# Both ends of a graph-attention kernel: a tile-wise start with three weight sums on GpSimd, row statistics on ScalarE, and a rearranged last block

## The chip, the cores and the metric

The kernel runs on one core of a Trainium2 chip, all in float32. The metric is the device time of one execution in microseconds (us). Lower is better. Before the change it was 2791.11 us, the median of 3 runs (2790.47 to 2792.8). Faster or slower needs a difference of 2%, which is 56 us here. The change aims at far less, so most of this study is about single microseconds, and about which of them are the kernel's and which are chance.

The engines are called as in the profile: PE (matmuls), DVE (vector), ACT (scalar), POOL (GpSimd), SP (issues transfers). Ratios are the mean time of one kernel's fast runs over the mean of the other's fast runs of the same rounds, so they are not quite the ratio of the medians quoted beside them.

## The reference, cut to what matters

```python
h = jnp.maximum(_layernorm(x, axis=-1), 0.0)          # x: 128 x 64 x 768, cut into 16 blocks of 512 rows
for l in range(2):
    m_left  = einsum('bsh,oh->bso', h, W_left[l])     # 768 x 768 weights
    m_right = einsum('bsh,oh->bso', h, W_right[l])
    u = ...                                           # h @ m_left^T, h @ m_right^T / sqrt(768), masked by adj
    attention = exp(u) * adj / (row sum + 1e-10)
    h_lin = einsum('bsh,oh->bso', h, W_lin[l]) + b_lin[l]
    h = relu(_layer_norm(attention @ h_lin, ln_a[l], ln_b[l]))
return x + h
```

## The kernel before: the parts that matter

Each 768x768 weight is cut into 3x3 blocks of 256, and a fast matrix-product scheme forms 15 block products from sums of weight blocks (`w_l`, `w_r`) and sums of token blocks (`ts`). I call the 15 products of block 0's left weight P0 to P14; the 15 of its right weight follow, then block 1. A product is added into bank X, Y, Z or V of PSUM, and "reads" by ACT and DVE gather the banks into `m`. The work beside the matmuls is hung on numbered slots of the product loop (`put(slot, ...)`, two slots a product).

The start (cut):

```python
# block 0: for each of four 128-row tiles q: statistics (DVE), root (ACT), inverse and shift (DVE), norm (ACT)
for q in range(Q):
    todo.extend(stats[q + 1:q + 2] + [scales[q], norms[q]])
...
def turn(c0):                     # two 128-column chunks of ALL four tiles: needs the last norm
    for c in range(2):
        for q in range(Q):
            nc.tensor.transpose(p[:, c, q * P:(q + 1) * P], xr[q][...], ident)
    ... nc.scalar.copy(ht[...], p[...])
...
t, w = deque(sums_t((1, 0, 0), nc.vector)), deque(sums_w(0, "l", nc.vector))     # all sums on DVE
needs = ("twww", "t", "wt", "ttwww", "wwww", "w", "tw", "t", ...)                # which sums before which product
# GpSimd: the 17 w_r sums for the right half, held back to slot 16
put(16, hold)
for n in range(0, len(rs), 3):
    put(17 + n // 3, *rs[n:n + 3])
```

Block 1's rows get their statistics on DVE during P8 to P13, are normalised on ACT, transposed on DVE, stored to DRAM as `h` and read back as `ht` (I call this the reload). GpSimd then makes the first token sums of block 1.

The end: the last block is computed in two halves of its rows. After each half its attention context is formed on PE, then squares and root on ACT, scaling on DVE, the addition of `ln_b` on GpSimd, relu and residual on DVE, and four stores on one queue.

## Time and profile before

| what | before |
|---|---|
| time, median of 3 | 2791.11 us |
| span of the profiled execution | 2791.6 us |
| PE busy | 99% of the span |
| first product P0 | 20.57 us |
| block 1's first product | 81.17 us |
| from the last half's first product to the end | 2791.6 - 2756.80 = 34.8 us |

Two views: the table of PE's waits, which tells for whom PE stood idle and how long, and the timeline, in which each row is a run of like instructions, with the start, the time from the first's start to the last's end, the count, and in brackets the idle time before it with what ended it.

### The profile page before, as it was taken

To read this page: it belongs to the slowest core of one execution; us is meant where nothing else is said; L and a number is where in the kernel's file an instruction comes from. 1 tells how busy PE (TensorE), PEld (TensorE's weight loads), DVE (VectorE), ACT (ScalarE), POOL (GpSimd) and SP (SyncE) were. 2 spreads that over 40 slices of the span, in tenths; PEclk is the share of its full clock that TensorE was granted. 3 is DMA by queue.
4 is the path that set the end of the run, shared out by engine and by line. 5 is a ranking of instruction groups with operands and counts; after the bars stand their busy time and mean duration, and the time that the engine had idled before them with its cause. 6 is when DMAs were issued, how large, how long until landed. Compare 5 with 4: busy or idle time off the path is not lost.

```text
span 2791.6 us, 46094 instructions
## 1 busy us (share of the span) xinstructions
PE 2751.3 (99%) x18712; PEld 2340.8 (84%) x18712; DVE 1340.8 (48%) x2215; ACT 837.8 (30%) x1453; POOL 1191.5 (43%) x935
## 2 busy tenths in 40 slices
PE   7999999999999999999999999999999999999997
PEld 6888888888888888888788888888888888888885
DVE  6455545454444332332345444544444335666666
ACT  2122222222231244444521211222121214445443
POOL 3332343223322456556432344223222325887875
PEclk9999999999999999999999999999999999999999
DMA  5533443344332243343555433443344204555654
GB/s 165 152 83 74 108 111 77 74 97 121 79 74 76 84 140 110 113 149 106 149 134 128 116 78 74 97 120 79 74 92 120 62 25 146 167 167 159 184 162 125
DMA packets 234068, 310.80 MB, mean 111 GB/s; under 512 B 54144, under 2 KB 184448, under 8 KB 225664
## 3 DMA queue, kind: packets, MB, share of 16 engines
q1 hardware_dynamic: 233568, 307.06, 41.5%
q8 instruction: 149, 2.44, 0.4%
q10 hardware_dynamic: 288, 0.79, 0.1%
q14 instruction: 63, 0.52, 0.1%
HBM read 202.91 MB, written 104.86 MB: 110 GB/s over the span
## 4 chain that ended last, share of the span: by engine, by line
PE 95%; issue 1%; DVE 1%; POOL 1%; DMA 1%; ACT 1%; SPq 0%; DVEq 0%; ACTq 0%; POOLq 0%
PE X L369 23%; PE V L369 15%; PE X L648 12%; PE Y L369 12%; PE Z L369 8%; PE V L648 8%; PE Y L648 6%; PE aux L395 5%; PE Z L648 4%; PE aux L575 3%; POOL w_r L145 1%; DVE wm L409 0%; DMA x<-in_x_dram 0%; DMA w_r<-in_w_right_dram 0%; DMA w_l<-in_w_left_dram 0%
## 5 line engine op out<-in xcount | busy, mean ns | idle before, releaser
L145 POOL TENSOR_TENSOR ts<-ht 128x512 f32<-128x512 f32 x441 | 586.4, 1341 | 1232.2 <-DMA ht<-h 567.6
L190 ACT ACTIVATE m<-X 128x512 f32<-128x512 f32 x256 | 152.5, 596 | 1106.7 <-PE X L369 582.4
L145 POOL TENSOR_TENSOR ts<-ht,ts 128x512 f32<-128x512 f32 x189 | 249.3, 1327 | 154.7 <-PE X L648 76.9
L145 DVE TENSOR_TENSOR m<-m,V 128x512 f32<-128x512 f32 x256 | 174.2, 680 | 269.5 <-PE V L369 269.4
L145 DVE TENSOR_TENSOR m<-m,X 128x512 f32<-128x512 f32 x256 | 163.7, 681 | 248.7 <-PE X L369 248.0
L369 PE MATMUL X<-ts,w_l 128*128 128x256 f32 x1024 | 244.7, 382 | 3.8 <-DVE w_l L145 2.1
L648 PE MATMUL X<-w_n,ts 128*128 128x256 f32 x1024 | 244.0, 380 | 0.8 <-ACT hl L190 0.6
L369 PE MATMUL X<-ts,w_r 128*128 128x256 f32 x1024 | 241.9, 379 | 0.0
L145 DVE TENSOR_TENSOR m<-m,Z 128x512 f32<-128x512 f32 x128 | 87.9, 687 | 313.4 <-ACT m L190 254.8
L369 PEld LDWEIGHTS X<-ts,w_l 128*128 128x128 f32 x1024 | 193.0, 191 | 35.5 <-DVE m L145 3.1
L648 PEld LDWEIGHTS X<-w_n,ts 128*128 128x128 f32 x1024 | 191.7, 190 | 31.7 <-DVE hl L145 1.8
L369 PEld LDWEIGHTS X<-ts,w_r 128*128 128x128 f32 x1024 | 192.3, 190 | 28.7
L256 ACT ACTIVATE ht<-ht,b_col,a_col 128x512 f32<-128x512 f32 x192 | 143.5, 804 | 142.6 <-DMA ht<-h 142.6
L648 PE MATMUL Y<-w_n,ts 128*128 128x256 f32 x768 | 182.4, 379 | 0.0
L369 PE MATMUL Y<-ts,w_l 128*128 128x256 f32 x768 | 181.4, 379 | 0.0
L369 PE MATMUL Y<-ts,w_r 128*128 128x256 f32 x768 | 181.4, 379 | 0.0
L190 ACT ACTIVATE hl<-X 128x512 f32<-128x512 f32 (+1 forms) x136 | 77.8, 572 | 329.2 <-PE X L648 326.3
L369 PEld LDWEIGHTS Y<-ts,w_r 128*128 128x128 f32 x768 | 145.9, 190 | 19.8
L369 PEld LDWEIGHTS Y<-ts,w_l 128*128 128x128 f32 x768 | 145.9, 190 | 19.8
L648 PEld LDWEIGHTS Y<-w_n,ts 128*128 128x128 f32 x768 | 145.9, 190 | 19.8
L614 POOL TENSOR_TENSOR z<-z,b 128x768 f32<-128x768 f32 x64 | 115.7, 1822 | 94.4 <-DVE z L611 94.4
L145 DVE TENSOR_TENSOR hl<-hl,X 128x512 f32<-128x512 f32 (+1 forms) x136 | 83.1, 652 | 146.6 <-PE X L648 141.8
(106 smaller groups left out, 4682.7 us busy)
## 6 DMA issues: line engine op xcount, KB each, us to landing
ht<-h SPq DMA_DIRECT2D x63, 1536.0 KB, 7.3
h<-xb SPq DMA_DIRECT2D x124, 384.0 KB, 6.4
z<-z SPq DMA_DIRECT2D x128, 192.0 KB, 2.9
x<-z SPq DMA_DIRECT2D x128, 192.0 KB, 8.5
xr<-in_x_dram SPq DMA_DIRECT2D x128, 192.0 KB, 3.7
out_dram<-xr SPq DMA_DIRECT2D x128, 192.0 KB, 2.6
x<-in_x_dram SPq DMA_DIRECT2D x120, 192.0 KB, 8.7
adj<-in_adj_dram SPq DMA_DIRECT2D x64, 128.0 KB, 2.7
```

What stands on the lines that cost most here:

```text
L145: (eng.tensor_add if sign == "+" else eng.tensor_sub)(o, a, b)
L190: nc.scalar.activation(to(o), p, AF.Copy, scale=1.0 if sign == "+" else -1.0)
L256: nc.scalar.activation(ht, ht, AF.Relu, bias=cols[1][:, c:c + 1], scale=cols[0][:, c:c + 1])
L369: nc.tensor.matmul(p[:, g], w[ORDER[i][0]][:, c, g * P:(g + 1) * P], b()[t][:, c, :], start=(new and g == c == 0), stop=(c == K2 - 1), ski ...
L395: nc.tensor.matmul(p[h * S + e:h * S + e + 32, q, e:e + 96], ht[:, c, b * S + e:b * S + e + 32], mb[:, e:e + 96], start=(c == 0), stop=(c ...
L575: nc.tensor.matmul(cx[k][i, m, :HH], at[j, q, :], hl[j, q, m * HH:(m + 1) * HH], start=True, stop=True)
L614: nc.gpsimd.tensor_add(zs[k], zs[k], rows["b"])
L648: nc.tensor.matmul(p[:, n], b[t][:, c, r * P:(r + 1) * P], w[s][:, c, :], start=(i in FIRST and i not in PRELOAD and n == c == 0), stop=(c ...
```

## The change

It aims at the two ends alone. The start: norms in a software pipeline, transposes tile by tile into all banks, three of the weight sums on GpSimd behind the last row scale. Block 1's statistics go from DVE to ACT (a sum pass and a squares pass). The end: the context of the last block earlier, residuals prefetched, `ln_b` folded in ahead (`max(z*r, -b) + (x + b)`), each tile stored on two queues. The core of the diff:

```diff
-            def turn(c0):
-                p = ps_aux.tile([P, 2, T], F32, name="aux")
-                for c in range(2):
-                    for q in range(Q):
-                        nc.tensor.transpose(...)
+            def turn(n, q):                       # one tile, six chunks, two banks
+                ... aux halves for n < 2, then banks X, Y and Z, V
+                for m, p in enumerate(banks):
+                    for c in range(3):
+                        nc.tensor.transpose(p[:, c * P:(c + 1) * P], xr[q][...], ident)
+                (nc.vector.tensor_copy if n < 2 else nc.scalar.copy)(...)
...
+                ws, vs = sums_w(0, "l", nc.gpsimd), sums_w(0, "l", nc.vector)
+                hold(KEEP["nb"][:, START[-1]:START[-1] + 1])
+                for f in ws[:3]:
+                    f()
-                needs = ("twww", "t", "wt", "ttwww", "wwww", "w", ...)
+                needs = ("tw", "wt", "t", "ttww", "wwww", "w", ...)
...
+            if u == 1:                            # block 1's statistics on ACT
+                todo.extend([lambda q=q: sums(q, total, func=AF.Copy) for q in range(Q)])
+                todo.append(lambda: nc.scalar.mul(total, total, -1.0 / H))
+                todo.extend([lambda q=q: sums(q, ss, func=AF.Square, bias=total[:, q:q + 1]) for q in range(Q)])
+                todo.extend([inverse, None] + norms)     # inverse: root on ACT, reciprocal and nb on DVE
...
+            def last_block(u): ...                # residual loads at slots 1 and 20, + ln_b on GpSimd at 22 and 40
+            def finish_last(u, r): ...            # squares, scaling, max, add, stores on two queues
-                    linear(u, (1,), 30, {4: ((u, 0), (50, 51, 52, 56, 58))}, ())
+                        ends = (..., {2: ((u, 0), (44, 45, 47, 61, 62))})      # in the last block
```

## The prediction

> **What bounds the kernel now.** I read the page first (busy shares, slices, chain), then the waits of PE, then the timeline of the first 100 us and of the last 35, since the change touches only those.
>
> ```profile
> PE 2751.3 (99%) x18712; PEld 2340.8 (84%) x18712; DVE 1340.8 (48%) x2215; ACT 837.8 (30%) x1453; POOL 1191.5 (43%) x935
> PE   7999999999999999999999999999999999999997
> ```
>
> PE is busy all through; only the first and last slice (70 us each) show less. So only time before, between and after the matmuls at the two ends can be won, and 2% (56 us) is out of reach. The waits of PE over the whole run, and the timeline of the start:
>
> ```profile
> PE aux L297 <- ACT x L276: 12.3, 4, 8.9
> PE X L369 <- DVE w_l L145: 2.9, 2, 2.1
> PE V L369 <- DVE m L145: 1.5, 1, 1.5
> PE X L369 <- POOL ts L145: 1.1, 1, 1.1
> ...
> 13.71 4.74 PE L297 MATMUL aux<-ident,x 128*128 128x128 f32 x21 [1.16 <-ACT x L276]
> 18.50 2.01 DVE L145 TENSOR_TENSOR w_l<-w_l,w_l 128x512 f32<-128x512 f32 x3
> 20.57 3.78 PE L369 MATMUL X<-ts,w_l 128*128 128x256 f32 x8 [2.12 <-DVE w_l L145]
> 48.68 1.99 PE L369 MATMUL Z<-ts,w_l 128*128 128x256 f32 x8 [0.92 <-DVE ts L145]
> 52.18 1.99 PE L369 MATMUL V<-ts,w_l 128*128 128x256 f32 x8 [1.51 <-DVE m L145]
> 57.54 5.23 SPq L313 DMA_DIRECT2D h<-xb  x4
> 68.02 0.35 SPq L249 DMA_DIRECT2D ht<-h  x1
> 79.85 2.49 POOL L145 TENSOR_TENSOR ts<-ht 128x512 f32<-128x512 f32 x2 [16.87 <-DMA ht<-h]
> 81.17 1.99 PE L369 MATMUL X<-ts,w_l 128*128 128x256 f32 x8 [1.10 <-POOL ts L145]
> ```
>
> The reader sees the first real product at 20.57 us, after all four tiles were normalised, transposed (until 18.45), copied, and summed on DVE. Dense products start 1.727 us apart (15 of them from 113.28 to 139.18), so block 0's 30 need 51.8 us; from 20.57 they end at 79.92, 7.5 us more: 3.1 in the first two (they start 3.57 and 2.96 apart), 0.98 at the fifth, 1.15 and 1.77 at the last two of the left half, crumbs. Then block 1 waits for its own h: stored at 57.54, reloaded at 68.02, summed on GpSimd from 79.85, first product 81.17. The end:
>
> ```profile
> 2777.91 0.81 ACT L601 ACTIVATE z<-aux 128x768 f32<-128x768 f32 x1 [11.31 <-PE aux L575]
> 2780.44 1.94 DVE L611 SCALAR_TENSOR_TENSOR z<-aux,rs,a 128x768 f32<-128x768 f32 x2
> 2781.61 3.56 POOL L614 TENSOR_TENSOR z<-z,b 128x768 f32<-128x768 f32 x2 [7.02 <-DVE z L611]
> 2783.44 3.41 DVE L626 SCALAR_TENSOR_TENSOR xr<-z,xr 128x768 f32<-128x768 f32 x2 [1.06 <-POOL z L614]
> 2786.01 2.42 SPq L628 DMA_DIRECT2D out_dram<-xr  x4
> ```
>
> PE's last context ends at 2778.48; 13.1 us of row work and stores follow. Before that, PE lost 0.83 (last product) and some 2 us between the last context's parts, because DVE stood at a residual waiting 1.9 us for its DMA with two reads queued behind it.
>
> **What the Trainium skill says.** "SBUF — State Buffer", section "Who interferes with whom": a DVE instruction with two SBUF inputs and a GpSimd instruction that reads SBUF exclude each other; with a PSUM operand it doesn't. The trace agrees mostly: the residual (two SBUF inputs) takes 944 ns alone and 2.54 us at 2783.44 beside GpSimd; the scaling out of PSUM takes 1.01 us always. One pair near 50.3 us shows no delay, so it isn't every time. "TensorE: Matmul & The Clock Gate", Part 1: an idle array runs at half clock until about 3.4 us of sustained work. The 3.57 us of the first product are twice 1.727; agrees. "ScalarE: Activation LUTs", "What ACT_TABLE_LOAD costs": 186 ns + 0.833 ns per element, 93 more per pointer operand: 0.83 us for a plain 768-element pass; the norm with two pointers shows 1.03 (1.01 by the page).
>
> **The change, part by part.** P0 to P14 are the products of the left half of block 0.
>
> 1. Pipelined norms. Before, a tile's turn is 1.63 us (norms at 7.73, 9.36, 11.00, 12.63) because root, inverse and norm wait for each other. Now the next tile's root stands ahead of a norm and its statistics ahead of the inverse; a turn is then the larger of ACT's 0.93+0.28 and DVE's 1.2+0.3, about 1.4. The first tile lands alone on one queue, where two shared the rate before: I take 4.3 us in place of 5.08 (estimate from 400 GB/s and 0.39 MB a tile). Last norm ends near 12.1 (was 13.66).
>
> 2. Tile-wise transposes. Only six of 24 are left after the last norm: 1.3 us, copies of 0.45 to 0.55 each, the last near 14.2. The first two tiles are the first token half, so the first sum of tokens runs near 13 us, before that.
>
> 3. Three weight sums on GpSimd, released by the last inverse (near 10.6): 3 x 1.27 us and starts, 4.1, end 14.8. DVE's two-SBUF sums fall into this; shutting out costs up to a sum or two (0.6 each). P0 starts near **15.6**, 5.0 earlier.
>
> 4. P0 and P1 cold as before (3.1 lost; the transposes, here already in pieces, did not warm it before). The four-sum wait before P4 is untouched (0.8 to 1.0).
>
> 5. Row statistics of block 1 leave DVE (eight of 0.51 us, four of 0.21, and the 1.02 us scale step caught by GpSimd) for ACT: 4 x 0.85 + 0.3 + 4 x 0.93 + 0.3, near 8 us, from P7's read at 33.9, then norms 4 x 0.95, done near 46.5. ACT has no read until the right half's first, at 47.1. The waits of 1.15 and 1.77 and 0.4 of crumbs go: P14 ends at 15.6 + 15 x 1.727 + 3.1 + 0.9 = **45.5** (was 53.91): 8.4 earlier.
>
> 6. But the transposes of block 1 now stand in right-half slots, one of them behind the read of its second product: P14's end + 0.7, three of 0.95, wait for that read to 50.2, the fourth to 51.1. The store is at P14's end + 5.7, before + 3.6. From store to reload, sums and product took 81.17 - 57.54 = 23.6; so block 1 starts at 51.2 + 23.6 = **74.8**, while PE is free at 45.5 + 25.9 = 71.4. The wait of 1.1 grows to 3.4. Net gain of the start: 81.17 - 74.8 = **6.4**, not 8.4.
>
> 7. The middle: the order of instructions stays, and PE is full. 0.
>
> 8. The last block. The context of the first rows comes after the third product (was the fifth), its residuals only after the last read: the wait for their DMA leaves DVE's path. From the second half's first product at 2756.80: 15 x 0.865, a context of 1.6, 0.4 of bank waits: last product ends 2771.8 (was 2773.6), read 2772.3, last context ends 2773.9 (was 2778.48): 4.6 earlier. Then DVE: two residuals to 2774.3 (GpSimd quiet, 0.95 each), two products with a 0.95 each to 2776.2, steps 0.45, max 1.0, add 0.9, again 0.4, 1.0, 0.9: 2780.9. ACT's squares and roots (2.4) hide. One issue on each of two queues, and 3.7 us from the last issue to the end as before (2787.88 to 2791.6): 2784.7. Gain **6.9**.
>
> Sum 13.3; I give back 0.7 for waits not seen: 2791.1 - 12.6 = **2778.5 us**.
>
> **Rivals.** (a) *The start gains nothing beyond block 1's wait.* Its h chain hangs on store, reload and GpSimd; if transposes or norms slip 2 us more, the start is worth 4: 2781. For: it binds before too (1.10 behind GpSimd). Against: ACT's norms have 1 to 3 us of slack. And if ACT's passes, in order, hold back the right half's first reads, PE stalls for banks too: 2782. (b) *Port exclusion*: the GpSimd sums and DVE's first sums shut each other out, P0 starts at 17: 2780. Against: the held start keeps them off the statistics, and PSUM copies don't take the port. (c) *The slowed clock returns* in the 3.4 us gap before block 1: up to 1.7 lost. The gap of 1.1 caused none. (d) *The end is bound by DVE alone* whatever PE does: its last chain is 8.6 us of DVE; were a residual's transfer still in its way, only 4 is gained: 2781. (e) The block-1 wait may be smaller, if the reload is quicker than 11.8 us (most take 7.3): 2775.
>
> **Range and chances.** Terms: first product +-1, clock +-1.2, store-to-reload +-1.5, end +-1.3, noise +-1; in quadrature near 2.7, for 8 in 10 near 3.5 to 4.5. Range **2774.0 to 2783.0**. Ratio 0.9955: within 2% 0.985, faster 0.007, slower 0.008.
>
> **What would show it right or wrong.** First real product at 15 to 17 us; left half ending near 45.5 without the two waits; ACT full from 34 to 46; store near 51; a wait of PE for GpSimd near 3.4 before block 1's first product at about 75; the middle shifted and otherwise alike; last context to end of span 10.8 (before 13.1), no DVE wait for xr. Wrong if: the first product waits for GpSimd's third sum beyond 17; ACT's statistics run past 48 and delay bank reads; x of block 1 lands after 34; or the wait before block 1 isn't there, so that the start gains 8.4.

## The result, and the profile after

The changed kernel took 2777.91 us, the median of 4 runs (2777.19 to 2780.4), beside 2791.45 for the kernel before in 4 runs. The ratio is 0.9953, 95% interval 0.9936 to 0.997: within 2%, as predicted, and 0.6 us from the predicted 2778.5. The sum came out right, but several of its terms did not. PE's waits after, whole run (engine, bank and line, for whom; us in total, times, longest):

```profile
PE aux L333 <- ACT x L283: 8.7, 2, 7.8
PE Z L408 <- issue: 1.7, 1, 1.7
PE X L408 <- POOL w_l L145: 1.7, 1, 1.7
PE V L408 <- DVE m L145: 1.4, 1, 1.4
PE X L408 <- DVE w_l L145: 1.4, 1, 1.4
```

The wait for the norms is shorter (8.7 for 12.3), the wait of P13 is gone, and so is block 1's wait for GpSimd's token sums. But P14's wait for DVE's read of `m` (1.5 before) is still there, and P4's wait for a weight sum (part of the 2.9 before) has become 1.4. The timeline of the start:

```profile
12.97 0.57 PE L333 MATMUL Z<-ident,x 128*128 128x128 f32 x3
13.37 0.49 PE L333 MATMUL V<-ident,x 128*128 128x128 f32 x3
15.55 1.99 PE L408 MATMUL X<-ts,w_l 128*128 128x256 f32 x8 [1.69 <-POOL w_l L145]
17.38 1.91 PE L408 MATMUL Z<-ts,w_l 128*128 128x256 f32 x8
24.15 1.97 PE L408 MATMUL X<-ht,w_l 128*128 128x256 f32 x8 [1.41 <-DVE w_l L145]
43.27 1.99 PE L408 MATMUL V<-ts,w_l 128*128 128x256 f32 x8 [1.42 <-DVE m L145]
50.98 4.79 SPq L352 DMA_DIRECT2D h<-xb  x4
60.80 0.35 SPq L251 DMA_DIRECT2D ht<-h  x1
67.84 2.50 POOL L145 TENSOR_TENSOR ts<-ht 128x512 f32<-128x512 f32 x2 [12.33 <-DMA ht<-h]
71.00 1.24 PE L408 MATMUL X<-ts,w_l 128*128 128x256 f32 x5
```

P0 starts at 15.55 (predicted 15.6). P1 follows after 1.83 us, not after the 3.57 of before: the clock is already up. The store is at 50.98 (predicted 51.2). Block 1's sums start 7.04 us after the reload was issued (11.83 before), so block 1 starts at 71.00 with no wait at all. The end:

```profile
2753.98 0.96 DVE L715 SCALAR_TENSOR_TENSOR xr<-z,xr 128x768 f32<-128x768 f32 x1 [1.41 <-POOL ht L647]
2758.18 1.13 PE L737 MATMUL X<-w_n,ts 128*128 128x256 f32 x4 [0.96 <-DVE hl L145]
2762.69 2.09 PE L621 MATMUL aux<-hl,at 64*64 64x384 f32 x16
2764.88 1.83 DVE L661 TENSOR_TENSOR z<-aux,a 128x768 f32<-128x768 f32 x2
2770.36 0.96 DVE L668 TENSOR_TENSOR ht<-ht,z 128x768 f32<-128x768 f32 x1
```

The last context ends at 2764.78, 18.0 us after the half's first product at 2746.78 (before 21.7); 10.6 us of row work and stores follow (before 13.1). Together 28.6 in place of 34.8: 6.2 us.

By these two traces the start gains 81.17 - 71.00 = 10.2 and the end 6.2, 16.4 us in all. That is more than the 13.5 between the medians. The reason is in the executions that were profiled: that of before took 2793.33 us, longer than each of its four timed runs, and that of after 2777.19, the shortest of its four. A part of what one trace shows is luck, and the experiments had to find out which part.

### The profile page after: what moved, and what is told of

It reads as the page before. It is cut to its first block, busy times and chain, and to the rows that moved or that the text cites. A ratio compares the mean times of both kernels' runs of the same rounds, so it can differ in the third digit from the quotient of the medians.

```text
span 2775.4 us, 46099 instructions
## 1 busy us (share of the span) xinstructions
PE 2744.7 (99%) x18712; PEld 2338.2 (84%) x18712; DVE 1338.8 (48%) x2208; ACT 843.6 (30%) x1469; POOL 1198.0 (43%) x940
## 4 chain that ended last, share of the span: by engine, by line
PE 97%; DVE 2%; ACT 1%; DMA 0%; issue 0%; SPq 0%; DVEq 0%; ACTq 0%
PE X L408 24%; PE V L408 16%; PE X L737 12%; PE Y L408 12%; PE Z L408 8%; PE V L737 8%; PE Y L737 6%; PE aux L434 5%; PE Z L737 4%; PE aux L621 3%; DMA w_l<-in_w_left_dram 0%; DVE ts L145 0%; DVE wm L448 0%; DVE m L145 0%; DVE w_l L145 0%
## 5 line engine op out<-in xcount | busy, mean ns | idle before, releaser
L408 PEld LDWEIGHTS X<-ts,w_r 128*128 128x128 f32 x1024 | 192.3, 190 | 28.7
L145 DVE TENSOR_TENSOR hl<-hl,V 128x512 f32<-128x512 f32 (+1 forms) x136 | 89.0, 655 | 127.8 <-PE V L737 127.3
```

The source lines that it names most:

```text
L145: (eng.tensor_add if sign == "+" else eng.tensor_sub)(o, a, b)
L408: nc.tensor.matmul(p[:, g], w[ORDER[i][0]][:, c, g * P:(g + 1) * P], b()[t][:, c, :], start=(new and g == c == 0), stop=(c == K2 - 1), ski ...
```

## The experiments

Twelve runs were made, in four calls, each on another chip and each with its own runs of the kernel before (medians 2790.72, 2790.76, 2793.41 and 2792.13 us). All gave the right result.

### First call: the parts apart

*after_again* is the changed kernel once more.

> The changed kernel unaltered. Time again 2777 to 2780. What is asked is its first products: in the one trace so far the first two start 1.83 and 1.75 us apart (full clock), in the kernel before 3.57 and 2.96 (half clock). Theory A, the clock's window is free-running and the start is lucky or unlucky: over the runs two groups some 3 us apart, and this trace may show 3.5 us spacings. Theory B, the new spacing of the transposes always releases the clock: all traces show 1.8, and the runs lie within 1.5 us. Also asked: reload of block 1's h in 7.0 us as in the first trace or 11.8 as before the change; no wait of PE in front of block 1's first product if 7.0, some 3 us if 11.8.

Measured: 2775.92 us (2775.02 to 2777.43), ratio 0.9947, interval 0.9934 to 0.9961. P0 at 15.00, P1 1.83 later, P4's wait 1.40, P14's 1.42, reload to sums 7.17, block 1 at 70.44 without a wait. Every feature of the first trace is there again.

*end_only* is the kernel before with the new last block alone.

```diff
  (kernel before)
+            def last_block(u): ...
+            def finish_last(u, r): ...
+                        ends = (..., {2: ((u, 0), (44, 45, 47, 61, 62))})
```

> The kernel before with the new last block alone. Theory: the end is worth 6.2 us of its own (from the second half's first product to the end of the span 28.6 us in the changed trace, 34.8 before): 2785.2, ratio 0.9978. Tail after the last context 10.6, was 13.1; last context 3.7 earlier. Rival: only the tail counts, since the time PE gains before is eaten by DVE's queue: 2.5 us, 2789.

Measured: 2784.11 us (2784.01 to 2784.69), ratio 0.9977, interval 0.9965 to 0.999: 6.6 us less than the before of its call. From the half's first product to the end it took 28.3 us. But its start, which is the old one, was quicker than in the first trace of before:

```profile
20.50 3.78 PE L369 MATMUL X<-ts,w_l 128*128 128x256 f32 x8 [2.11 <-DVE w_l L145]
67.76 0.35 SPq L249 DMA_DIRECT2D ht<-h  x1
74.69 2.50 POOL L145 TENSOR_TENSOR ts<-ht 128x512 f32<-128x512 f32 x2 [11.97 <-PE Y L369]
```

The reload took 6.9 us, not 11.83, and block 1 began at 79.65 without a wait. So the wait of 1.1 us in the first trace of before does not belong to every execution of the old start.

*start_stats* is the change without the new last block, and *start_only* is the same with block 1's statistics back on DVE.

```diff
  (start_stats, against the change)
-                    else:
-                        last_block(u)
+                    (the last block as before)
  (start_only, also)
-            if u == 1:
-                ... sums(q, total, func=AF.Copy), sums(q, ss, func=AF.Square, ...)
+            if u:
+                for f in stats + [lambda: [f() for f in scale(0, Q)]]: ...
```

> The change without its new last block: first block tile by tile, GpSimd sums, statistics of block 1 on ScalarE. Theory: the start is worth what the trace shows up to block 1's first product, 81.2 to 71.0, so 10 us if the clock is released early, 7 if not: 2781 to 2784.5. Rival: block 1's wait for its own h takes back all above 6.4 us, as predicted: 2785.

> As start_stats, but with the row statistics of block 1 back on VectorE. Theory from the prediction: the waits of 1.2 and 1.8 us at the end of the left half come back, 2.5 to 3 us slower than start_stats to the end of the left half, though the store of h stands two slots earlier. Rival: the changed trace still has a wait of 1.42 there with the statistics on ScalarE, so VectorE's wait for GpSimd's port is the cause and the statistics are worth under 1.5 us.

Measured: start_stats 2782.79 us (2781.18 to 2784.25), ratio 0.9972, interval 0.9959 to 0.9984; start_only 2784.13 (2782.39 to 2785.36), ratio 0.9976, interval 0.9964 to 0.9989. With the statistics on DVE the waits of before are back:

```profile
41.51 1.99 PE L390 MATMUL Z<-ts,w_l 128*128 128x256 f32 x8 [0.92 <-DVE ts L145]
45.02 1.99 PE L390 MATMUL V<-ts,w_l 128*128 128x256 f32 x8 [1.51 <-DVE m L145]
```

From P0 to P14 it took 29.26 us here and 27.73 in start_stats. So the statistics on ACT are worth 1.5 us in the traces: P13's wait and small remainders, not both waits. The medians differ by 1.3 us the same way, but the two ranges overlap, so the times alone do not show it. The parts add up: 7.9 for the start with statistics and 6.6 for the end make 14.5, and the whole change took 14.8 off in the same call.

### Second call: the clock, the port, the end's wait

In all four traces with the new start so far the first two products had been quick (1.83 and 1.75 us apart), and in both of the old start slow. To see whether PE's idle gap before P0 is the reason, *before_warm* fills it in the kernel before with dummy transposes, and *before_again* is the kernel before for a second trace.

```diff
  (before_warm, against the kernel before, behind the last transpose)
+            def keep_busy():
+                p = ps_st.tile([P, 2 * TH], F32, name="V")
+                for n in range(9):
+                    nc.tensor.transpose(p[...], xr[3][...], ident)
```

> The kernel before, with nine dummy transposes (some 0.216 us each, 1.94 us in all, result never read) put on PE after its last real transpose, in the gap of 2.1 us in which PE waits for the first weight sums. Theory A (the clock is released after 5 to 6 us of PE work without a gap above some 1.3 us, transposes counting): PE is then busy from 13.7 us on, the clock is released near 19 to 20 us, the first two products start 1.75 to 1.85 us apart instead of 3.57 and 2.96, and the time falls by some 2.5 to 3 us, to about 2788. Rival B (transposes don't count, and the change is warm early for another reason, such as its three-piece order or bank use): the first two products stay at 3.57 and 2.96, and the time stays within 0.5 us of 2790.7, or rises by a few tenths if the dummies hold up the first product.

> The kernel before, unchanged, for a second trace. Theory A: the first two products are cold again (3.57 and 2.96 apart), so the clock is no matter of luck. For the reload of block 1's h, which took 11.8 us in the first trace of before and 7.0 us in all four traces of variants: if it was a chance event of that one trace, it takes about 7 us here, block 1 starts without its wait of 1.1 us, and the span is 2789 to 2791; if it belongs to the kernel, it is near 11.8 again with a wait near 1.1.

Measured: before_again 2789.94 us in its one run, before_warm 2790.87 (2790.29 to 2793.34), ratio 1.0002, interval 0.999 to 1.0015. First before_again, then before_warm:

```profile
13.74 4.02 PE L297 MATMUL aux<-ident,x 128*128 128x128 f32 x21 [1.16 <-ACT x L276]
20.60 3.52 PE L369 MATMUL X<-ts,w_l 128*128 128x256 f32 x8 [2.83 <-DVE w_l L145]
23.95 1.89 PE L369 MATMUL Z<-ts,w_l 128*128 128x256 f32 x8
```

```profile
13.79 4.30 PE L297 MATMUL aux<-ident,x 128*128 128x128 f32 x21 [1.16 <-ACT x L276]
17.93 1.15 PE L309 MATMUL V<-ident,x 128*128 128x128 f32 x9
20.64 1.99 PE L376 MATMUL X<-ts,w_l 128*128 128x256 f32 x8 [1.57 <-DVE w_l L145]
22.48 1.89 PE L376 MATMUL Z<-ts,w_l 128*128 128x256 f32 x8
```

In the first trace of before the same 21 transposes took 4.74 us; here they took 4.02 and 4.30, so the clock came up during the transposes. In before_again it fell back in the gap of 2.83 us, and P0 took 3.35 us to P1. In before_warm the gap left was 1.57, and P0 and P1 ran at full speed. That a filled gap keeps the clock up fits theory A, in one trace, with one correction: my count of 5 to 6 us of work was wrong, since the same kernel came up at different times. And its time did not fall: the loss of 1.6 to 3.1 us at P0 was avoided, but this trace's reload took 10.82 us and block 1 started at 77.81, only 0.7 before before_again. With an interval of 2.5 thousandths (7 us) wide, a gain of a us or two would not show; whether there is one stays open.

*split_hold* tests P14's wait. In the change GpSimd runs 17 `w_r` sums from 32.13 us for 23.39 us. By "the port" I mean what the prediction quotes: GpSimd's reads and DVE's sums of two SBUF inputs exclude each other. Beside GpSimd's sums those of DVE look like this (trace of the changed kernel, DVE):

```profile
37.99 1.80 DVE L145 TENSOR_TENSOR ts<-ht 128x512 f32<-128x512 f32 x1
40.32 1.16 DVE L145 TENSOR_TENSOR ts<-ht 128x512 f32<-128x512 f32 x1
41.60 1.02 DVE L300 TENSOR_TENSOR nb<-total,rs 128x4 f32<-128x4 f32 x1
42.54 0.67 DVE L145 TENSOR_TENSOR m<-m,V 128x512 f32<-128x512 f32 x1
```

The last line is the read that P14 waits for. The scale step `nb` has 4 elements a row and takes 1.02 us. The experiment stops GpSimd in this stretch:

```diff
-                        for n in range(0, len(rs), 3):
-                            put(17 + n // 3, *rs[n:n + 3])
+                        put(17, *rs[:4])
+                        put(25, lambda: hold(M[0][:, 0, 4, 0, :1]))
+                        put(26, *rs[4:])
```

> The changed kernel, with the seventeen w_r sums of GpSimd in two lots: four at the old place (31.4 us), the other thirteen held until the read of the thirteenth product (near 40 us). Theory A (the wait of 1.42 us before the last left-half product is DVE standing for the SBUF port that GpSimd's sums hold): DVE's token sum of 1.80 us and its row scale of 1.02 us fall to about 0.68 and 0.2, that wait goes to nearly 0, the left half ends 1.3 to 1.5 us earlier, and the time falls by 1.0 to 1.5 us to about 2774.5 to 2775. Rival B (DVE simply has too much work there, or the bank is held by another reader): the wait stays above 1 us and the time within 0.5 us of after. Rival C (the later sums are late for the right half): PE waits over 0.5 us for w_r in the right half's first five products, and the gain is lost.

Measured: 2773.69 us (2772.34 to 2776.44), ratio 0.994, interval 0.9926 to 0.9954. Its DVE and PE:

```profile
39.00 0.68 DVE L145 TENSOR_TENSOR ts<-ht 128x512 f32<-128x512 f32 x1
41.00 0.16 DVE L300 TENSOR_TENSOR nb<-total,rs 128x4 f32<-128x4 f32 x1
41.08 0.68 DVE L145 TENSOR_TENSOR m<-m,V 128x512 f32<-128x512 f32 x1
```

```profile
40.77 1.89 PE L408 MATMUL Z<-ts,w_l 128*128 128x256 f32 x8
42.50 1.89 PE L408 MATMUL V<-ts,w_l 128*128 128x256 f32 x8
```

The sums fell to 0.68, the scale to 0.16, and P14 follows P13 after 1.73 us, without a wait. In the right half PE waits nowhere for `w_r`. So P14's wait in the changed kernel comes from GpSimd's sums beside DVE's, and DVE's amount of work (rival B) is not the cause. P5 to P14 took 15.54 us here and 17.32 in late_add of the same call: 1.8 us. The medians of the two are 4.5 us apart, more than the mechanism gives; the rest is not explained by it.

*late_add* tests the wait of 0.96 us in the last half, which the profile puts down to DVE, and behind it to GpSimd's addition of `ln_b` (the bracket at 2753.98 above).

```diff
-                for xs, slot in zip(XS[u, 1], (22, 40)):
+                for xs, slot in zip(XS[u, 1], (22, 52)):
```

> The changed kernel, with the last block's second GpSimd addition moved from the second half's sixth place to its twelfth (slot 40 to 52). Theory A (the last half's wait of PE for DVE, 1.0 us before its eleventh product, comes from a row addition on DVE that waits 1.4 us for GpSimd): the wait falls below 0.3, the last context ends some 0.8 to 1.0 us earlier, the time falls by 0.5 to 1.0 us. Rival B (the scaling behind it is bound by ScalarE's squares and root instead): the wait stays near 1 us, the time unchanged.

Measured: 2778.21 us (2775.76 to 2778.67), ratio 0.9953, interval 0.994 to 0.9965. A miss:

```profile
2755.39 0.96 DVE L715 SCALAR_TENSOR_TENSOR xr<-z,xr 128x768 f32<-128x768 f32 x1 [1.43 <-DMA xr<-in_x_dram]
2759.59 1.13 PE L737 MATMUL X<-w_n,ts 128*128 128x256 f32 x4 [0.98 <-DVE hl L145]
```

GpSimd is out of the way, and DVE waits as long as before, now for the transfer of the residual `xr`. GpSimd's end and the transfer's landing had been close together, and the bracket names only the later one. ScalarE (my rival B) was not it either.

### Third call: the residual, the clock held up, and the parts together

*early_xr* loads that residual at the last block's start instead.

```diff
                 put(1, lambda: load(1))
+                put(3, lambda: residual(u - 1, 1))
...
-                        if k and u + r < NB - 1:
+                        if k and u + r < NB - 1 and (u, r) != (NB - 2, 0):
```

> The changed kernel, with the residual rows of the second-last block's second half loaded at the last block's start (place 3) in place of behind the row work of its first half (place 21, issued at 2749.95 us of the trace of late_add, landing near 2755.3). Theory A (the wait of PE for DVE in the last half, 0.98 us, comes from DVE standing at that residual for its transfer): the idle time of DVE before it falls from 1.4 us to below 0.3, PE's wait before its eleventh product falls below 0.4, the last context ends 0.6 to 1.0 us earlier against the second half's first product, and the time falls by as much against after (to some 2775.5 to 2777). Rival B (DVE's row work is bound by ScalarE's root and by slot order): the wait stays at 0.7 or more, the time is the same.

Measured: 2777.13 us (2776.67 to 2780.28), ratio 0.9945, interval 0.9932 to 0.9959; the change's own ratio was 0.9953 and 0.9947, so in time no gain can be told.

```profile
2752.82 1.91 DVE L716 SCALAR_TENSOR_TENSOR xr<-z,xr 128x768 f32<-128x768 f32 x1 [0.17 <-issue]
2757.98 1.13 PE L738 MATMUL X<-w_n,ts 128*128 128x256 f32 x4 [0.67 <-DVE hl L145]
```

The idle time before the residual went from 1.4 to 0.17 us, but the instruction itself now takes 1.91 instead of 0.96, because GpSimd's addition stands beside it again (2752.09 to 2753.91 us). PE's wait is 0.67, between the two theories, but no gain can be read from that: in the six traces that have the new last half with neither edit, the same wait is 0.66 to 1.04 us (0.67 in end_only and split_hold). Both causes are seen there too. The transfer ends DVE's idle time in end_only, split_hold and sums_dve (0.97 to 1.21 us), GpSimd's addition in the two traces of the changed kernel (1.41 and 1.49), and in warm_after, where DVE did not wait for the transfer, its instruction took 1.82 us. So the transfer and the port both stand in this place, and either can fill it. Removing both was not run.

*warm_after* is the changed kernel with dummy transposes of the identity from 1.3 us on, between the tiles, and up to the first product.

```diff
+            todo.append(lambda: keep_busy(v, 28))
             for n, q in enumerate(START):
                 todo.append(lambda n=n, q=q: turn(n, q))
+                if n < 2:
+                    todo.append(lambda n=n: keep_busy(v, (6, 4)[n]))
+            todo.append(lambda: keep_busy(ps_aux.tile(...)[:, 0], 8))
```

> The changed kernel, with dummy transposes of the identity (28 from 1.3 us on, 6 and 4 between the tiles' turns, 8 after the last) that keep PE busy from the start to the first product. Theory A (the granted clock is decided in steps of about 3.4 us on the share of the step in which PE is busy: in ten traces it rose after steps with 84% or more, stayed low after 79% or less, held at 50% and fell at 40%): the clock is up before the first product in every execution, the first two products start 1.84 and 1.73 us apart, the spread of the runs shrinks, and the time falls by 0.5 to 1 us on average against after (whose six traces lost 0.1 four times and 1.7 to 2.0 twice). Rival B (only real products count): the first two products are slow in some traces as before. Rival C: the dummies get in the way of the real transposes, the first product starts over 0.5 us later, and nothing is gained.

Measured: 2777.63 us (2775.99 to 2780.61), ratio 0.9946, interval 0.9933 to 0.9958.

```profile
1.34 4.88 PE L343 MATMUL V<-ident 128*128 128x128 f32 x28 [1.34 <-POOL floor L209]
14.36 1.99 PE L417 MATMUL X<-ts,w_l 128*128 128x256 f32 x8 [1.24 <-POOL w_l L145]
16.19 1.92 PE L417 MATMUL Z<-ts,w_l 128*128 128x256 f32 x8
22.96 1.96 PE L417 MATMUL X<-ht,w_l 128*128 128x256 f32 x8 [1.40 <-DVE w_l L145]
```

The clock was up from 4.67 us and the products are quick, as theory A said; the time and its spread are as without. Part of the reason is in the last line: where P0 and P1 run at full speed, P4 waits 1.40 us for DVE's weight sums, and where they run slow it waits 0.82 (late_add), so 0.6 us of any such gain ends there.

*best* has the three together.

```diff
+ (split_hold) + (early_xr) + (warm_after)
```

> The changed kernel with the GpSimd sums in two lots (as split_hold), the early residual (as early_xr) and the dummy transposes (as warm_after). If the three act on separate waits, their gains add: 1.4 + 0.8 + 0.6, about 2.8 us below after, near 2774 where after is 2776 to 2778. If the start is then held by block 1's own h (store, reload, GpSimd sums) a wait of PE for GpSimd comes back before block 1's first product and takes 0.5 to 1.5 of it.

Measured: 2776.89 us (2774.5 to 2778.36), ratio 0.9941, interval 0.9928 to 0.9953. Its trace has the quick start, no wait at P14, and block 1's first product at 68.74 us, 2.3 before the changed kernel's, with no wait for GpSimd. The wait I feared did not come. But the gains did not add in time: 0.9941 is not apart from the 0.9945 and 0.9946 of its own call, nor from split_hold's 0.994. A place where some of it goes is a gap in block 1's first scores or second product that the profile names "issue", its word for a wait without a recorded releaser: 2.13 us here and 2.60 in warm_after, 0.59 to 1.94 in the twelve other traces. The transfer packets kept with the traces suggest a cause. In all fourteen a 16-KB packet of the queue of instructions (not of data) ends shortly before, and PE starts again 1.27 to 1.52 us after its end (changed kernel: packet from 77.27 to 78.25 us, PE again at 79.77). So PE probably stood there for its next instructions; no run tests it.

### Fourth call: what the weight sums on GpSimd bring

The part of the change not yet tested apart was the move of three sums to GpSimd. *sums_dve* moves them back and leaves the rest.

```diff
-                ws, vs = sums_w(0, "l", nc.gpsimd), sums_w(0, "l", nc.vector)
-                hold(KEEP["nb"][:, START[-1]:START[-1] + 1])
-                for f in ws[:3]:
-                    f()
-                needs = ("tw", "wt", "t", "ttww", "wwww", ...)
+                t, w = deque(sums_t((1, 0, 0), nc.vector)), deque(sums_w(0, "l", nc.vector))
+                needs = ("twww", "t", "wt", "ttwww", "wwww", ...)
```

> The changed kernel with the first three weight sums back on DVE, in the order of the kernel before; GpSimd does nothing until its w_r sums. In the traces of the change the three sums run on GpSimd from 10.75 to 14.94 us (trace of after_again), and DVE's first token sum takes 1.46 in place of 0.68 us and its next two weight sums 2.35 in place of 1.28, so GpSimd's work costs DVE 1.8 us, what three sums of 0.6 us would cost it. Theory A (the move brings nothing, for it is paid back at the port): the first product starts within 0.5 us of 15.0, the fifth (which waits for DVE) within 0.5 us of 23.6, and the time is within 1 us of after. Theory B (the move brings what the prediction's step 3 meant, the sums beside the transposes): the first product starts at 16.3 or later, and the time rises by 1 us or more against after.

Measured: 2776.79 us (2776.49 to 2780.41), ratio 0.9948, interval 0.9935 to 0.9962, the same as the change's. The changed kernel's GpSimd and DVE first, then those of sums_dve:

```profile
11.31 4.18 POOL L145 TENSOR_TENSOR w_l<-w_l,w_l 128x512 f32<-128x512 f32 x3
12.91 1.46 DVE L145 TENSOR_TENSOR ts<-ht 128x512 f32<-128x512 f32 x1
14.29 2.35 DVE L145 TENSOR_TENSOR w_l<-w_l,w_l 128x512 f32<-128x512 f32 x2
```

```profile
12.34 0.69 DVE L145 TENSOR_TENSOR ts<-ht 128x512 f32<-128x512 f32 x1
12.94 2.01 DVE L145 TENSOR_TENSOR w_l<-w_l,w_l 128x512 f32<-128x512 f32 x3
15.10 1.96 PE L408 MATMUL X<-ts,w_l 128*128 128x256 f32 x8 [1.23 <-DVE w_l L145]
```

P0 starts at 15.10 us and P4 at 23.55, against 15.00 and 23.60 in after_again. GpSimd's three sums cost DVE 1.8 us of blocking, as much as DVE needs to do them itself. This part of the change brings nothing that these runs can show.

### The clock, over all fourteen traces

The traces also record when PE's granted clock changed. All its changes lie on a grid of 3.413 us, whose phase differs from run to run. I took PE's busy share in each step of the grid over the first 30 us:

| what the clock did at the end of a step | PE's busy share in that step |
|---|---|
| was at half, stayed | all at 79% or less (before: 79%, 60%, 78%; split_hold: 73%, 69%) |
| was at half, rose | all at 84% or more (after: 84%; before_again: 92%; start_only: 90%) |
| was at full, stayed | all at 51% or more (after: 51%; before_warm: 54%) |
| was at full, fell | 26% (before_again), 40% (late_add), 45% (early_xr) |

Over these 30 us the four groups do not overlap in any of the traces, so a start is quick or slow by where the grid falls on the kernel's pattern of work and gaps. Over the whole span they do overlap: the clock held after steps with 47% (best, near 78 us) and 50% (after, near 81 us), and in the last context of the old end it fell after steps with 56% (before_again, before_warm, start_only). So the shares of the table are no thresholds, and PE's busy share is not all that decides. In before_again and before_warm that fall came in the middle of the last context, and from the last half's first product to the end they took 35.7 us, where the three other traces with the old end took 34.8. The nine traces with the new end took 28.3 to 28.7.

The loss at P0 and P1 (start of P2 less start of P0 less 2 x 1.727) was 3.1, 2.9 and 1.6 us in the three traces with the old start; with the new start and no dummies it was 0.1 in five traces (after, after_again, start_stats, start_only, sums_dve) and 2.0, 1.7 and 1.8 in three (split_hold, late_add, early_xr). On average that is 2.5 against 0.8. This difference, 1.8 us before P4 takes its part, is an estimate from eleven traces. It belongs to the change, whose transposes begin earlier and whose gap before P0 is shorter, but no single execution is sure to get it.

## Why the prediction was right or wrong, point by point

- **What bounds the kernel**: right. PE is at 99% before and after, and only the two ends moved.
- **Steps 1 and 2, pipelined norms and tile-wise transposes**: right. P0 came 5.0 us earlier, as said. sums_dve shows that these two steps give nearly all of it.
- **A reading of the port**: wrong. The "pair near 50.3 us" of before that "shows no delay" is a DVE sum at 50.29 that takes 1.24 us, where the same form takes 0.68 at 47.94. With the scale step at 48.75 (1.02 us) it stands just before the wait of P14, so the trace already pointed to what step 5 missed.
- **Step 3, sums on GpSimd**: the number (P0 at 15.6, measured 15.55) was right and the reason incomplete. I charged the port with "a sum or two (0.6 each)". It was 1.8 us, three sums, and the move has no worth.
- **Step 4, "P0 and P1 cold as before (3.1 lost)"**: wrong by 3.0 us in this trace. The sentence that the transposes "did not warm it before" took one trace for a rule. P4's wait was not untouched either: it grew from 0.98 (start to start) to 1.56, as P4 came to DVE's sums sooner.
- **Step 5, statistics on ACT**: half right. ACT ran them from 31.8 us, with no delay to the reads of banks (the second half of rival a); the norms stood 3.04 us for DVE's scale step and still ended at 46.4 for a predicted 46.5. Of the waits "of 1.15 and 1.77", P13's went and P14's stayed, at 1.69 start to start. split_hold shows why: with the statistics gone, what is left is GpSimd's sums shutting DVE out. (GpSimd stopped with the statistics still on DVE was not run.) The step is a wait that I ascribed to the wrong neighbour. The left half still ended at 45.0 us for a predicted 45.5, because +3.0 from the clock met -0.6 at P4 and -1.7 at P14.
- **Step 6, block 1's wait of 3.4 us**: wrong. The store came at 50.98 (said 51.2), but the 23.6 us from store to product contained a reload of 11.83. It was 6.8 to 7.4 us in the ten traces with the new start; with the old start it was 11.83, 10.82, 7.2 and 6.9. The term was mis-sized by 4.8 us, which rival e had named, and the gain of the start was 7.9 us in time (start_stats) in place of 6.4. Why the reload is slow in two of four old starts is open, but the packets in the traces show where: of its 128 packets of 12 KB the last starts 5.4 to 5.7 us after the issue in the twelve quick reloads, while in the slow ones the last four (before) or three (before_warm) start one by one until 10.2 and 8.6 us after it, when the next block's rows are already being loaded.
- **Step 7, the middle**: unchanged as far as can be seen. From block 1's first product to the last half's first it took 2674.0 to 2676.6 us in the traces without dummies in the new start, with or without the change, and 2676.2 and 2677.7 in best and warm_after, which have the longest gaps named "issue".
- **Step 8, the end**: right in kind and a little too high: 6.9 predicted, 6.2 in the trace and 6.6 in the medians of end_only. The tail after the last context was 10.6 us for a predicted 10.8. The last context came 3.7 us earlier, not 4.6, because of a DVE wait before the eleventh product (0.96), which the transfer of a residual and GpSimd's port cause between them.
- **Rivals**: (a) did not come true; (b) did not move P0 but is right on the port; (c), a clock that falls in the gap before block 1, could not arise, since the gap went away; (d) did not come true.
- **The sum**: 13.3 less 0.7 was predicted. Measured were 13.5 between the medians of the result and 14.8 between those of the first call. Steps 4 and 6 were too low (by 3.0 and 3.4), step 5 with P4's wait and step 8 too high (by 2.3 and 0.7). In the two traces these errors do not cancel: their spans differ by 16.2, which is 3.6 more than the 12.6 predicted. The medians differ by less, and the trace of before on which the prediction was built was a slow execution (2793.33) with the slowest reload of all. So it is partly luck that the hit is within 0.6 us.

## What to carry to other kernels

Before reading single microseconds off one trace, take a second trace of the same kernel: here a slow transfer, the phase of the clock and a slow execution had together put several us into the first that the kernel did not own. Here, moving work to GpSimd beside a DVE that sums two SBUF operands was no overlap: count what DVE loses, and look for waits elsewhere (P14's) that are really the same port. Where a wait has two causes that end close together, the profile names one, and taking that away shows the other; test until the wait itself is gone.

## What the Trainium skill lacked or had wrong

- "TensorE: Matmul & The Clock Gate", Part 1, gives a free-running window of 3413 ns, and a fall of the clock after a window of idleness. The runs agree on the grid: the clock's changes lie 3.413 us or a multiple apart in all fourteen traces. What the page lacks are the shares. In the first 30 us the clock rose only after a step with PE busy 84% or more (not at 79%), held at 51% or more, and fell in steps with 45%, 40% and 26%, so with gaps of only 1.89, 2.12 and 2.83 us (early_xr, late_add, before_again). Later in the span it held at 47% and fell at 56%, so the busy share of the profile is not the whole rule.
- The same page, Part 4, says that transposes do not count as PE-busy in the same way and do not bring the full clock. In warm_after 28 transposes of the identity alone brought it at 4.67 us, and in before_again 21 transposes took 4.02 us in place of 4.74 as it rose among them. The trace records them as matmuls against an identity and does not tell whether they ran in the transpose mode that the page means.
- "SBUF — State Buffer", "Who interferes with whom", is borne out: DVE sums of two SBUF inputs took 1.16 to 1.80 us beside GpSimd and 0.68 alone, a 4-element scale 1.02 and 0.16, and reads with a PSUM operand 0.67 either way. What it lacks is the balance: three sums of 1.4 us on GpSimd cost DVE 1.8 us, what it needs for the three itself.
- No page that I read gives a figure for the scatter of a transfer within a kernel: the reload of the same 1.5 MB takes about 7 us in twelve traces and 10.8 and 11.8 in two, in which only its last three or four packets are late.
